# Buffers, order and lag operations in a fused attention and feed-forward layer on one core

## The chip, the cores and the metric

The kernel runs on one core of one Trainium2 chip. A core has five engines that run their own instruction lists: TensorE (PE in the profile, with PEld for its weight loads), VectorE (DVE), ScalarE (ACT), GpSimd (POOL) and SyncE (SP). POOL and SP issue nearly all transfers here; SP's queue is written SPq. The metric is the device time of one execution in microseconds. Before the change the median of three executions was 1432.9 us (1429.92 to 1437.33).

## The reference

One layer over 2048 tokens of width 512, all in float32. After a layer norm come a short recurrent attention with 16 heads of 128 and a feed-forward part with weights reduced to their signs, and both meet at the end.

```python
q = _silu(x @ Wq); k = _silu(x @ Wk); v = _silu(x @ Wv)
z = x @ Wz; a = x @ Wa; b = x @ Wb
q, k, v = (_causal_dwconv(u, w) for u, w in ...)      # 4 taps
q = q * cos + rot_half(q) * sin                       # k likewise
q = q / jnp.maximum(jnp.linalg.norm(q, axis=-1, keepdims=True), 1e-12)   # k likewise
for s in range(4):                                    # lags
    attn = jnp.einsum('bshd,bshd->bsh', q, _lag(k, s)) * scale
    gate = jax.nn.sigmoid(_lag(a, s) * b)
    out = out + (attn * gate)[..., None] * _lag(v, s)
rms = jax.lax.rsqrt(jnp.mean(out * out, axis=-1, keepdims=True) + EPS_NORM)
s = (out * rms * norm_w * _silu(z)) @ Wout
hidden = jax.nn.relu((xn @ sign(up).T) * up_scale)
g = _silu((hidden @ sign(down).T) * down_scale * output_scale)
return x + s * g
```

## The kernel before

Tokens lie along the free axis, channels on the 128 partitions. The 2048 tokens are four blocks of 512 (`b`, `TB`), the 16 heads eight pairs (`p`, `NP`); a pair is 256 channels, two tiles `j` of 128. The normalised and transposed input `xnT` of all blocks stays in SBUF, each row with three zero columns ahead of it (`HALO`), for the lags.

`step(p, b)` (L604) is the unit of work. It computes q and k of pair p for block **b + 1** (`queries`, `products`) and v, z and the output of pair p for block **b**. So the first pass, b = -1, has only q and k, and beside them runs the feed-forward part of block 0 (`ups`, `downs`), whose raw weights are loaded, turned into signs and stored for later (`fetch`, L699). The last block (L765 to L828) has only v, z and the output, in a loop of its own, and behind it comes the feed-forward part of blocks 1 to 3.

For a pair, PE multiplies `xnT` by the pair's weights (16 records of a 128x512 matmul for each of q, k, v, z, under the names pq, pk, pv, pz), ACT takes the SiLU out of PSUM into a "raw" tile, ACT and DVE apply the four taps (`convolve`, L322: one ACT multiply at L325 and three DVE operations per half). `turn` makes from q the three turned copies for lags 1 to 3; `products` (L366) multiplies them by k at four shifts (`pr`), and PE sums over channels into a PSUM bank "dots" (`sum_dots`). The squares of q and k go the same way into "squares" (`sum_squares`).

Once per block, at p = 0, `norms` (L469) takes the squares out of PSUM into `r`, via a copy `sq2` (L475); `norms_in_rows` (L482) takes reciprocals and spreads them by eight small DMAs on SP into `rk` and `rq`; `coefficients` (L496) multiplies dots, norms and gates, and stores them in DRAM (`co_dram`). `gate_products` (L231, at p = 7) and `gate` (L251, at p = 1) prepare the gates: PE makes four partial sums, ACT copies them to `ab_sb`, and POOL adds them in DRAM by a chain of four DMAs (L247, L249), each waiting for the one before; sixteen DMAs on SP bring them back. The tiles ab_sb, gate_b, sq2 and rk share **one** buffer, tag "rk".

`weighted` (L525) brings the coefficients back from DRAM, repeated over partitions (`bc`, two lags to a tile, three buffers), multiplies them with v at four shifts and adds (`te`, `o`). `gated_output` (L556) multiplies with z (`oz`), and for every two pairs `output_projection` (L570) adds four PSUM tiles (po) to the result in DRAM. At p = 0 the output of the pair (`out_of`) is put off to the next step, in `first_due`, since its coefficients have just been computed; its z is not.

The order of work: PE and DVE keep the order of the program text (the wrapper `InOrder`), and so does POOL for the add of squares, and SP in the last block. What is left on ACT, SP and POOL is ordered by the framework's planner before the program runs. Every engine then works its list in order, so an instruction that waits holds all behind it. Buffers are given per tag; with `bufs=1` the next writer waits for the last reader of the same tag.

Of the kernel before, what the change touches and what calls it, by code (L numbers as in the profile page):

```python
# [38 lines left out]
F32 = mybir.dt.float32  # L39
# [5 lines left out]
P = 128  # L45
# [36 lines left out]
def recurrent_layer(ctx: ExitStack, tc: tile.TileContext, a: dict, out: bass.AP):  # L82
# [148 lines left out]
    def gate_products(b):  # L231


        chunks = mm.tile([P, TB], F32, tag="mm", name=f"ab{b}")
        for k in range(KC):
            pe.matmul(
                chunks[LW * k : LW * k + LW, :],
                w_ab[:, k, :],
                xnT[:, k, HALO + b * TB : HALO + (b + 1) * TB],
                start=True,  # L240
                stop=True,
                tile_position=(0, LW * k),
            )
        ab = qks.tile([P, TB], F32, tag="rk", name=f"ab_sb{b}", bufs=1)
        nc.scalar.copy(ab, chunks)
        to = ab_dram[:, HALO + b * TB : HALO + (b + 1) * TB]
        nc.gpsimd.dma_start(to, ab[0:LW, :])  # L247
        for k in range(1, KC):
            nc.gpsimd.dma_start(to, ab[LW * k : LW * k + LW, :], accum_op=ALU.add)  # L249

    def gate(b):  # L251

        g = qks.tile([P, TB], F32, tag="gate", name=f"gate{b}", bufs=1)
        other = qks.tile([P, TB], F32, tag="rk", name=f"gate_b{b}", bufs=1)
        for r in range(0, P, H):
            lo = HALO + b * TB - r // LW
            nc.sync.dma_start(g[r : r + H, :], ab_dram[0:H, lo : lo + TB])
            nc.sync.dma_start(other[r : r + H, :], ab_dram[H:, HALO + b * TB : HALO + (b + 1) * TB])
        dve.tensor_tensor(g, g, other, ALU.mult)
        nc.scalar.activation(g, g, AF.Sigmoid)  # L260
        gates[b] = g
# [104 lines left out]
    def products(p, b, q, between=None, beside_k=None):  # L366
# [43 lines left out]
        if not b:  # L410
# [35 lines left out]
    def sum_dots():  # L446
# [4 lines left out]
        for pr in prs:  # L451
            for s in range(LAGS):
                src = pr[:, LAGS - 1 - s, :]
                add(banks["dots"], s, heads, src, p == 0, last and pr is prs[-1])

    def sums_of_o(b):

        so = mm.tile([P, TB], F32, tag="mm", name=f"so{b}")
        for j in range(2):
            add(so, j, ones, squares[b][:, j], True, True)  # L460
        row = vs.tile([P, HID], F32, tag="part", name=f"so_sb{b}", bufs=3)
        nc.scalar.copy(row[0 : 2 * LW], so[0 : 2 * LW])  # L462
# [6 lines left out]
    def norms(b):  # L469

        sqs = banks["squares"]
        r = qks.tile([P, HALO + TB], F32, tag="r", name=f"r{b}", bufs=1)[0 : 2 * LW]
        nc.scalar.copy(r[0:LW, 0:HALO], kept_r)
# [8 lines left out]
    def norms_in_rows(b):  # L482
# [7 lines left out]
        for s in range(LAGS):  # L490
            at = slice(LW * s, LW * s + LW)
            nc.sync.dma_start(rq[at, :], r[LW :, HALO:])
            nc.sync.dma_start(rk[at, :], r[0:LW, HALO - s : HALO - s + TB])
        rows[b] = rk, rq
# [12 lines left out]
    def values(p, b, raw):  # L507
# [4 lines left out]
        return v  # L512

    def load_wo(p, b):
        wo = vs.tile([P, 2, HID], F32, tag="wo", name=f"wo_{p}_{b}", bufs=3)
        loads["by"].dma_start(wo, a["wo"][p])
        return wo

# [6 lines left out]
    def weighted(p, b, v):  # L525

        n = f"_{p}_{b}"
        o = vs.tile([P, 2, TB], F32, tag="o", name="o" + n, bufs=1)
        for s in range(LAGS):
            if s % 2 == 0:  # L530

                bc = vs.tile([P, 2, TB], F32, tag="bc", name=f"bc{s}" + n, bufs=3)
                for h in range(2):
                    row = co_dram[b][s : s + 2, 2 * p + h, :]
                    loads["by"].dma_start(
                        bc[h * D // 2 : (h + 1) * D // 2], row.partition_broadcast(D // 2)
                    )
            b2 = bc[:, s % 2].unsqueeze(1).to_broadcast([P, 2, TB])
            v_s = v[:, :, HALO - s : HALO - s + TB]
            if s == 0:  # L540
                dve.tensor_tensor(o, v_s, b2, ALU.mult)
            else:
                te = vs.tile([P, 2, TB], F32, tag="te", name=f"te{s}" + n, bufs=2)
                dve.tensor_tensor(te, v_s, b2, ALU.mult)
                dve.tensor_tensor(o, o, te, ALU.add)

# [9 lines left out]
    def gated_output(p, b, o, z, wo):  # L556
# [6 lines left out]
        gated[p] = oz, wo  # L563
        if p % 2 == 1:
            pairs = gated.pop(p - 1), gated.pop(p)
            outputs_due.append(lambda midway: output_projection(p, b, midway, *pairs))
        if p == NP - 1:
            outputs_due.append(lambda midway: sums_of_o(b))

    def output_projection(p, b, midway, *pairs):  # L570

        for c in range(TC):
            if midway and c == TC // 2:
                midway()
            po = mm.tile([P, HID], F32, tag="mm", name=f"po{c}_{p}_{b}")
            for i, (of, w) in enumerate(pairs):
                for j in range(2):
# [23 lines left out]

    first_due = []

    def step(p, b, beside_q=None, beside_k=None):  # L604
# [30 lines left out]
        if at:  # L635
            load(vs, "z", p, b)
            wo = load_wo(p, b)
            z = gates_of_output(p, b)
            out_of = lambda: gated_output(p, b, weighted(p, b, v), z, wo)
# [39 lines left out]

    def up_projection(ph, pool, f, b, up_f, xs):  # L680
        for k in range(KC):
            for i, term in enumerate(xs):
# [6 lines left out]
                )  # L689
        hid = pool.tile([P, TB], F32, tag="hid", name=f"hid{f}_{b}", bufs=3)  # L690
        nc.scalar.activation(hid, ph, AF.Relu, scale=up_scale[:, f : f + 1])  # L691
# [4 lines left out]
    with tc.tile_pool(name="pre", bufs=1, side="right") as pre:  # L696
        signs = {}

        def fetch(g, which):  # L699

            for f in range(G * g, G * g + G):
                raw = pre.tile([P, HID], F32, tag="raw", name=f"pre_{which}_raw{f}", bufs=4)
                src = a[which][f]
                nc.sync.dma_start(raw, src.rearrange("p k m -> p (k m)") if which == "up" else src)
                sign = pre.tile([P, HID], F32R, tag="sign", name=f"pre_{which}{f}", bufs=8)

                (act if f < G else nc.scalar).activation(sign, raw, AF.Sign)
                nc.gpsimd.dma_start(signs_dram[which][:, f], sign)
                signs[which, f] = sign

        hids = {}

        def ups(lo, hi):
            for f in range(lo, hi):
                up_f = signs.pop(("up", f)).rearrange("p (k m) -> p k m", k=KC)
                ph = mm.tile([P, TB], F32, tag="mm", name=f"ph{f}")
                hids[f] = up_projection(ph, pre, f, 0, up_f, xs)

# [57 lines left out]
    load(vs, "v", 2, last)  # L776
    wo = load_wo(0, last)
    sum_dots()
# [21 lines left out]
    for p in range(NP + 1):  # L800
        if 1 < p < NP:
            weights["v"] = v_weights.pop(p)
            raw = raw_of(vs, "v", p, last, 1)
        if p:
            z = gates_of_output(p - 1, last)
# [9 lines left out]
        if p:  # L815
            gated_output(p - 1, last, o, z, wo)
# [211 lines left out]
```

## Time and profile before

| what | value |
|---|---|
| median of three runs | 1432.9 us |
| the profiled execution | 1432.86 us, span 1431.1 us |
| PE | 1405.0 us busy (98%), 3970 matmul records |
| DVE | 1209.8 us busy (85%), 1363 instructions |
| ACT | 611.6 us busy (43%) |
| POOL | 231.2 us busy (16%) |
| mean granted PE clock | 0.994 |

The span is the time from the first to the last instruction. An engine's busy time counts its instructions, not its waits. In the lists below "idle before <-releaser" is the time that the engine stood before an instruction, and what ended it. One logical float32 matmul shows as two records. The slices of the page, in tenths of 1/40 of the span, show PE full nearly throughout and DVE nearly so until the last quarter:

```profile
PE   9999999799999999999999999999998999999998
...
DVE  7899988999999979999999899999995978246454
```

### The profile page before, as it was taken

The numbers are of one execution on the slowest core, as the hardware profiler recorded it, in microseconds if no ns is written. First come the engines' busy times: TensorE is split into PE (matmuls) and PEld (weight loads), VectorE is DVE, ScalarE is ACT, GpSimd is POOL, SyncE is SP. The second block draws the span as 40 slices with busy tenths as digits, with TensorE's granted clock in tenths as the row PEclk, the third lists the DMA queues.
The fourth block names the chain that finished last, engine by engine and source line by source line (L and its number), as shares of the span: only waits on it lengthen the run. The fifth ranks groups of instructions, "written<-read, shape, count | busy, mean of one in ns | idle before, by whom it ended". The sixth has DMA issues, their size and how long they took to land.

```text
span 1431.1 us, 12627 instructions
## 1 busy us (share of the span) xinstructions
PE 1405.0 (98%) x3970; PEld 689.1 (48%) x3970; DVE 1209.8 (85%) x1363; ACT 611.6 (43%) x1181; POOL 231.2 (16%) x317
## 2 busy tenths in 40 slices
PE   9999999799999999999999999999998999999998
PEld 5554544344444444444444444444443444478886
DVE  7899988999999979999999899999995978246454
ACT  6575545445444443444434444444442333232122
POOL 2222120111212220112122201121211111200000
PEclk9999999999999999999999999999999999999999
DMA  9979576987998588779986798797748878662120
GB/s 308 269 194 213 151 198 139 228 211 185 192 220 198 135 176 235 199 167 203 214 201 150 165 238 194 179 204 175 167 87 219 221 209 200 130 232 89 33 88 30
DMA packets 101778, 259.22 MB, mean 181 GB/s; under 512 B 18832, under 2 KB 19344, under 8 KB 97360
## 3 DMA queue, kind: packets, MB, share of 16 engines
q0 software_dynamic: 33088, 104.89, 38.4%
q1 hardware_dynamic: 68624, 153.53, 35.5%
q8 instruction: 32, 0.52, 0.1%
q14 instruction: 34, 0.28, 0.1%
HBM read 157.67 MB, written 35.68 MB: 135 GB/s over the span
## 4 chain that ended last, share of the span: by engine, by line
PE 64%; DVE 20%; issue 7%; DMA 5%; ACT 2%; SPq 1%; POOL 1%; DVEq 0%; POOLq 0%; ACTq 0%
PE po L76 13%; PE pz L76 11%; PE pv L76 9%; PE pq L76 8%; PE pk L76 8%; PE pf L76 6%; PE ph L76 6%; DVE q L76 4%; DVE pr L76 3%; DVE k L76 2%; DVE te L76 2%; DVE o L76 2%; DVE v L76 2%; DMA ab_dram<-ab_sb 1%; DMA gate_b<-ab_dram 1%
## 5 line engine op out<-in xcount | busy, mean ns | idle before, releaser
L76 PE MATMUL po<-wo,oz 128*128 128x512 f32 x512 | 228.8, 601 | 10.5 <-DVE oz L76 10.5
L76 PE MATMUL pz<-xnT,wz 128*128 128x512 f32 x512 | 228.3, 599 | 4.5 <-DMA wz<-in_wz_dram 4.5
L76 PE MATMUL pq<-xnT,wq 128*128 128x512 f32 (+1 forms) x528 | 226.1, 580 | 0.9 <-ACT rk L274 0.9
L76 PE MATMUL pv<-xnT,wv 128*128 128x512 f32 x512 | 226.4, 594 | 0.0
L76 PE MATMUL pk<-xnT,wk 128*128 128x512 f32 x512 | 225.2, 592 | 0.0
L76 PEld LDWEIGHTS po<-wo,oz 128*128 128x128 f32 x512 | 97.0, 192 | 139.6 <-issue 112.7
L76 DVE SCALAR_TENSOR_TENSOR k<-rk,conv_w,k 128x512 f32<-128x512 f32 x192 | 141.9, 751 | 24.3 <-ACT k L325 19.8
L76 PEld LDWEIGHTS pz<-xnT,wz 128*128 128x128 f32 x512 | 97.4, 191 | 131.0 <-issue 128.9
L76 DVE SCALAR_TENSOR_TENSOR q<-rq,conv_w,q 128x512 f32<-128x512 f32 x192 | 141.3, 749 | 22.2 <-ACT q L325 17.7
L76 PEld LDWEIGHTS pq<-xnT,wq 128*128 128x128 f32 x528 | 99.0, 189 | 124.1 <-issue 115.2
L76 PEld LDWEIGHTS pv<-xnT,wv 128*128 128x128 f32 x512 | 95.7, 189 | 127.7 <-issue 117.8
L76 PEld LDWEIGHTS pk<-xnT,wk 128*128 128x128 f32 x512 | 96.6, 189 | 120.5 <-issue 116.9
L76 DVE SCALAR_TENSOR_TENSOR v<-rv,conv_w,v 128x512 f32<-128x512 f32 x192 | 141.3, 750 | 5.5 <-ACT v L325 1.0
L76 DVE SCALAR_TENSOR_TENSOR q<-q,turns 128x1024 f32<-128x1024 f32 (+1 forms) x128 | 127.1, 1013 | 2.3
L76 DVE TENSOR_TENSOR o<-o,te 128x1024 f32<-128x1024 f32 x96 | 117.6, 1225 | 3.3
L76 DVE TENSOR_TENSOR te<-v,bc 128x1024 f32<-128x1024 f32 x96 | 116.9, 1218 | 1.9 <-DMA bc<-co_dram 1.9
L76 DVE TENSOR_TENSOR pr<-q,k 128x2048 f32<-128x2048 f32 x52 | 117.3, 2286 | 0.9
L691 ACT ACTIVATE hid<-ph,up_scale 128x512 f32<-128x512 f32 x64 | 43.8, 685 | 120.0 <-PE ph L76 119.4
L76 DVE CAST hid_hi<-hid 128x512 fp32r<-128x512 f32 x64 | 27.1, 423 | 71.9 <-ACT hid L691 71.9
L76 PE MATMUL ph<-xs_hi,up 128*128 128x512 f32 x192 | 76.4, 398 | 0.7 <-ACT so_sb L462 0.7
L76 PE MATMUL ph<-xs_lo,up 128*128 128x512 f32 x192 | 75.9, 395 | 0.0
L586 ACT COPY part<-po 128x512 f32<-128x512 f32 x64 | 37.1, 581 | 90.4 <-PE po L76 53.7
(146 smaller groups left out, 1663.0 us busy)
## 6 DMA issues: line engine op xcount, KB each, us to landing
bc<-co_dram SPq DMA_DIRECT2D x128, 256.0 KB, 6.8
pr<-pr POOLq DMA_DIRECT2D x72, 256.0 KB, 6.0
wq<-in_wq_dram SPq DMA_DIRECT2D x32, 512.0 KB, 6.7
wk<-in_wk_dram SPq DMA_DIRECT2D x32, 512.0 KB, 6.6
sq<-sq POOLq DMA_DIRECT2D x32, 512.0 KB, 5.7
wv<-in_wv_dram SPq DMA_DIRECT2D x32, 512.0 KB, 6.1
wz<-in_wz_dram SPq DMA_DIRECT2D x32, 512.0 KB, 5.1
wo<-in_wo_dram SPq DMA_DIRECT2D x32, 512.0 KB, 6.5
```

The costliest lines, as they stand in the source:

```text
L76: return self.tc.keep_in_program_order(getattr(self.engine, op)(*args, **kwargs))
L586: nc.scalar.copy(part, po)
L691: nc.scalar.activation(hid, ph, AF.Relu, scale=up_scale[:, f : f + 1])
```

## The change

**Own buffers.** `ab_sb` gets its own tag "ab" instead of "rk". `r` gets two buffers instead of one, `part` (and the row of squares that shares it) four instead of three. `hid` gets two instead of three in the feed-forward part of blocks 1 to 3.

**z of a first pair.** At p = 0 the matmuls of z are no longer issued in step 0, but in step 1, between k and v (`z_due`).

**Two lags in one operation.** The four lags are stored in reverse (row group s holds lag 3 - s), so that two lags of v are one access pattern. `weighted` multiplies two lags at once and adds the two results in place; the square `o2` goes into a part of `xnT` that is no longer read, or (block 0) into the place of the second product. In `products` the second half of an odd pair is one multiply in place over q and one add, instead of two of each.

**Signs.** `fetch` only loads, into eight buffers instead of four, two steps ahead; `sign` makes the signs a step ahead.

**Last block.** z's weights of pair 1 are loaded before the coefficients are computed. The first output product moves from the third to the fourth turn of the loop, behind z of pair 3; wo of pairs 3 and 4 are then loaded together.

```diff
-        ab = qks.tile([P, TB], F32, tag="rk", name=f"ab_sb{b}", bufs=1)
+        ab = qks.tile([P, TB], F32, tag="ab", name=f"ab_sb{b}", bufs=1)
...
-            lo = HALO + b * TB - r // LW
+            lo = b * TB + r // LW
...
-            for lo in range(0, LAGS, 2):
-                half = qks.tile([P, 2, TB], F32, tag="half", name=f"half{lo}" + n, bufs=1)
-                product(half, 1, lo, lo + 2)
-                dve.tensor_tensor(pr[:, lo : lo + 2], pr[:, lo : lo + 2], half, ALU.add)
+            product(q[:, :, 1], 1, 0, LAGS)
+            dve.tensor_tensor(pr, pr, q[:, :, 1], ALU.add)
...
-        r = qks.tile([P, HALO + TB], F32, tag="r", name=f"r{b}", bufs=1)[0 : 2 * LW]
+        r = qks.tile([P, HALO + TB], F32, tag="r", name=f"r{b}", bufs=2)[0 : 2 * LW]
...
     def weighted(p, b, v):
...
+            v0 = v[:, :, lo : lo + TB]
+            v_lags = bass.AP(v0.tensor, v0.offset, [v0.ap[0], [1, 2], *v0.ap[1:]])
+            te = vs.tile([P, 2, 2, TB], F32, tag=f"te{lo}", name=f"te{lo}" + n, bufs=1)
+            dve.tensor_tensor(te, v_lags, bc.unsqueeze(2).to_broadcast([P, 2, 2, TB]), ALU.mult)
+            parts.append(te)
+        dve.tensor_tensor(parts[0], parts[0], parts[1], ALU.add)
+        o = parts[0][:, 0]
+        dve.tensor_tensor(o, o, parts[0][:, 1], ALU.add)
...
-            o2 = vs.tile([P, 2, TB], F32, tag="o2", name="o2" + n, bufs=1)
+            o2 = xnT[:, p % 2 * 2 : p % 2 * 2 + 2, HALO : HALO + TB] if b else parts[1][:, 0]
...
-            part = vs.tile([P, HID], F32, tag="part", name=f"part{c}_{p}_{b}", bufs=3)
+            part = vs.tile([P, HID], F32, tag="part", name=f"part{c}_{p}_{b}", bufs=4)
...
         products(p, b + 1, q, (lambda: norms_in_rows(b)) if change and b else None, beside_k)
+        if z_due:
+            z_due.pop()()
...
             if change:
+                z_due.append(z_of)
                 first_due.append(out_of)
             else:
+                z_of()
                 out_of()
...
-    def up_projection(ph, pool, f, b, up_f, xs):
+    def up_projection(ph, pool, f, b, up_f, xs, bufs=2):
...
-                raw = pre.tile([P, HID], F32, tag="raw", name=f"pre_{which}_raw{f}", bufs=4)
+                raw = pre.tile([P, HID], F32, tag="raw", name=f"pre_{which}_raw{f}", bufs=8)
...
+        groups = [(g, which) for g in range(NP // 2) for which in ("up", "down")]
+        fetch(*groups[0])
+        def first_signs():
+            sign(*groups[0])
+            fetch(*groups[1])
...
-                step(p, -1, lambda: fetch(0, "up"), lambda: ups(0, G))
+                step(p, -1, first_signs, lambda: ups(0, G))
...
-            if p < NP - 1:
-                fetch((p + 1) // 2, "down" if p % 2 == 0 else "up")
+            if p + 1 < NP:
+                sign(*groups[p + 1])
+            if p + 2 < NP:
+                fetch(*groups[p + 2])
...
-    wo = load_wo(0, last)
+    load_wo(0, last)
+    z_weights = {0: weights["z"]}
+    load(vs, "z", 1, last)
+    z_weights[1] = weights["z"]
     sum_dots()
     coefficients(last)
...
-        if p % 2 == 1:
+        if p % 2 == 1 and p != 3 or p == 4:
             output_projections()
+        if 1 < p < NP:
+            load(vs, "z", p, last)
+            z_weights[p] = weights["z"]
         if 0 < p < NP:
-            load(vs, "z", p, last)
             v = values(p, last, raw)
...
-        if 0 < p < NP:
-            wo = load_wo(p, last)
+        if p == 4:
+            load_wo(3, last)
+        if 0 < p < NP and p != 3:
+            load_wo(p, last)
```

More of the change, by code (lines that the diff above doesn't have):

```diff
@@ L452, in sum_dots @@
             for s in range(LAGS):
-                src = pr[:, LAGS - 1 - s, :]
-                add(banks["dots"], s, heads, src, p == 0, last and pr is prs[-1])
+                add(banks["dots"], s, heads, pr[:, s, :], p == 0, last and pr is prs[-1])
     def sums_of_o(b):
@@ L460, in sums_of_o @@
             add(so, j, ones, squares[b][:, j], True, True)
-        row = vs.tile([P, HID], F32, tag="part", name=f"so_sb{b}", bufs=3)
+        row = vs.tile([P, HID], F32, tag="part", name=f"so_sb{b}", bufs=4)
         nc.scalar.copy(row[0 : 2 * LW], so[0 : 2 * LW])
@@ L492, in norms_in_rows @@
             nc.sync.dma_start(rq[at, :], r[LW :, HALO:])
-            nc.sync.dma_start(rk[at, :], r[0:LW, HALO - s : HALO - s + TB])
+            nc.sync.dma_start(rk[at, :], r[0:LW, s : s + TB])
         rows[b] = rk, rq
@@ L512, in values @@
         return v
+    wos = {}
     def load_wo(p, b):
@@ L516, in load_wo @@
         loads["by"].dma_start(wo, a["wo"][p])
-        return wo
+        wos[p] = wo
     def gates_of_output(p, b):
@@ L527, in weighted @@
         n = f"_{p}_{b}"
[L528 to L545, printed above, removed]
+        parts = []
+        for lo in range(0, LAGS, 2):
+            bc = vs.tile([P, 2, TB], F32, tag="bc", name=f"bc{lo}" + n, bufs=3)
+            for h in range(2):
+                row = co_dram[b][lo : lo + 2, 2 * p + h, :]
+                loads["by"].dma_start(
+                    bc[h * D // 2 : (h + 1) * D // 2], row.partition_broadcast(D // 2)
+                )
+            v0 = v[:, :, lo : lo + TB]
[6 more added lines that the diff above has]
+        dve.tensor_tensor(o, o, parts[0][:, 1], ALU.add)
         if p == 0:
@@ L554, in weighted, with gated_output @@
         return o
-    def gated_output(p, b, o, z, wo):
+    def gated_output(p, b, o, z):
         oz = vs.tile([P, 2, TB], F32, tag="oz", name=f"oz_{p}_{b}", bufs=3)
@@ L562, in gated_output, with output_projection @@
             )
-        gated[p] = oz, wo
+        gated[p] = oz
         if p % 2 == 1:
             pairs = gated.pop(p - 1), gated.pop(p)
-            outputs_due.append(lambda midway: output_projection(p, b, midway, *pairs))
+            outputs_due.append(lambda midway: output_projection(p, b, midway, pairs))
         if p == NP - 1:
             outputs_due.append(lambda midway: sums_of_o(b))
-    def output_projection(p, b, midway, *pairs):
+    def output_projection(p, b, midway, pairs):
+        ws = wos.pop(p - 1), wos.pop(p)
         for c in range(TC):
@@ L575, in output_projection @@
             po = mm.tile([P, HID], F32, tag="mm", name=f"po{c}_{p}_{b}")
-            for i, (of, w) in enumerate(pairs):
+            for i, (of, w) in enumerate(zip(pairs, ws)):
                 for j in range(2):
@@ L602, in recurrent_layer @@
     first_due = []
+    z_due = []
     def step(p, b, beside_q=None, beside_k=None):
@@ L636, in step @@
             load(vs, "z", p, b)
-            wo = load_wo(p, b)
-            z = gates_of_output(p, b)
-            out_of = lambda: gated_output(p, b, weighted(p, b, v), z, wo)
+            load_wo(p, b)
+            z = []
+            z_of = lambda: z.append(gates_of_output(p, b))
+            out_of = lambda: gated_output(p, b, weighted(p, b, v), z[0])
             if change:
+                z_due.append(z_of)
                 first_due.append(out_of)
             else:
+                z_of()
                 out_of()
@@ L689, in up_projection @@
                 )
-        hid = pool.tile([P, TB], F32, tag="hid", name=f"hid{f}_{b}", bufs=3)
+        hid = pool.tile([P, TB], F32, tag="hid", name=f"hid{f}_{b}", bufs=bufs)
         nc.scalar.activation(hid, ph, AF.Relu, scale=up_scale[:, f : f + 1])
@@ L697, in recurrent_layer, with sign @@
         signs = {}
+        raws = {}
         def fetch(g, which):
             for f in range(G * g, G * g + G):
-                raw = pre.tile([P, HID], F32, tag="raw", name=f"pre_{which}_raw{f}", bufs=4)
+                raw = pre.tile([P, HID], F32, tag="raw", name=f"pre_{which}_raw{f}", bufs=8)
                 src = a[which][f]
                 nc.sync.dma_start(raw, src.rearrange("p k m -> p (k m)") if which == "up" else src)
[L705 to L709, printed above, removed]
+                raws[which, f] = raw
+        def sign(g, which):
+            for f in range(G * g, G * g + G):
+                of = pre.tile([P, HID], F32R, tag="sign", name=f"pre_{which}{f}", bufs=8)
+                (act if which == "up" and f < G else nc.scalar).activation(
+                    of, raws.pop((which, f)), AF.Sign
+                )
+                nc.gpsimd.dma_start(signs_dram[which][:, f], of)
+                signs[which, f] = of
         hids = {}
@@ L716, in ups @@
                 ph = mm.tile([P, TB], F32, tag="mm", name=f"ph{f}")
-                hids[f] = up_projection(ph, pre, f, 0, up_f, xs)
+                hids[f] = up_projection(ph, pre, f, 0, up_f, xs, 3)
         def downs(g, lo, hi):
@@ L804, in recurrent_layer @@
         if p:
+            weights["z"] = z_weights.pop(p - 1)
             z = gates_of_output(p - 1, last)
-        if p % 2 == 1:
+        if p % 2 == 1 and p != 3 or p == 4:
             output_projections()
+        if 1 < p < NP:
+            load(vs, "z", p, last)
+            z_weights[p] = weights["z"]
         if 0 < p < NP:
-            load(vs, "z", p, last)
             v = values(p, last, raw)
@@ L815, in recurrent_layer @@
         if p:
-            gated_output(p - 1, last, o, z, wo)
+            gated_output(p - 1, last, o, z)
         if p < NP:
             o = weighted(p, last, v)
-        if 0 < p < NP:
-            wo = load_wo(p, last)
+        if p == 4:
+            load_wo(3, last)
+        if 0 < p < NP and p != 3:
+            load_wo(p, last)
         if p < NP:
```

## The prediction

> **What bounds the kernel now.** I read the page's shares first (PE 98% busy, DVE 85%), then the stage table, which gives each engine's busy time in stretches that I cut at the same point of the loop (its columns: stretch, length, busy time and count of PE, PEld, DVE, ACT and POOL, granted clock, DMA share, GB/s).
>
> ```profile
> 209.00:300.00 91.00, 83.74 (x217) 34.91 (x217) 82.86 (x93) 42.24 (x87) 11.07 (x15) 0.94 0.76 192
> 371.50:442.50 71.00, 71.00 (x177) 30.35 (x177) 69.35 (x72) 30.96 (x64) 13.28 (x17) 1.00 0.97 211
> 515.70:589.20 73.50, 71.64 (x179) 30.62 (x178) 63.49 (x75) 32.93 (x68) 11.59 (x16) 1.00 0.79 209
> 1084.70:1161.00 76.30, 71.83 (x162) 31.39 (x161) 56.43 (x61) 21.68 (x40) 9.31 (x14) 0.96 0.82 217
> ```
>
> A stretch of two pairs (second row) is 71.0 us of PE in 71.0 us, with DVE only 1.65 us behind. The change takes no matmul away, so it can win only what PE loses: 7.26 us in the first block, 1.86 in the second, 4.47 in the last, and a clock below 1 in two of these stretches. PE's own list of waits and its order of time show where:
>
> ```profile
> PE po L76 <- DVE oz L76: 10.5, 3, 7.3
> PE pz L76 <- DMA wz<-in_wz_dram: 4.5, 1, 4.5
> ...
> 284.30 7.20 PE L76 MATMUL po<-wo,oz 128*128 128x512 f32 x10 [7.26 <-DVE oz L76]
> 575.70 1.55 PE L76 MATMUL po<-wo,oz 128*128 128x512 f32 x3 [1.86 <-DVE oz L76]
> 1103.19 9.92 PE L76 MATMUL pz<-xnT,wz 128*128 128x512 f32 x16 [4.47 <-DMA wz<-in_wz_dram]
> 1112.95 7.03 PE L76 MATMUL pv<-xnT,wv 128*128 128x512 f32 x16
> ```
>
> Sixteen records take 7.03 us at full rate, 0.43 each. After the 7.26 us wait ten take 7.20, that is 2.9 too many; after 4.47 us sixteen take 9.92, again 2.9; after 1.86 us three take 1.55, nothing extra. A long wait is paid twice. **What PE loses:** 7.26 + 2.9 = 10.2 (first block), 1.86 and 1.39 (second and third, the three waits of 10.5), 4.47 + 2.9 = 7.4 (last block), and 2.45 at 131 us, where five starts of pf that should be 0.233 apart cover 3.62 us behind hid_hi. Sum 23.3. That is the ceiling.
>
> **Who is late.** In the first three, oz comes from DVE, which runs its list in order without a gap up to the stall; so its last idle time before it counts. The orders of time of DVE and ACT:
>
> ```profile
> 217.57 2.33 DVE L76 SCALAR_TENSOR_TENSOR k<-rk,conv_w,k 128x512 f32<-128x512 f32 x3 [5.46 <-ACT k L325]
> 216.23 0.58 ACT L475 COPY sq<-squares 64x512 f32<-64x512 f32 x1 [4.69 <-DMA ab_dram<-ab_sb]
> ...
> 517.25 0.19 ACT L473 COPY r<-kept_r 32x3 f32<-32x3 f32 x1 [5.25 <-DMA rk<-r]
> 526.33 0.60 ACT L313 ACTIVATE rq<-pq 128x512 f32<-128x512 f32 x1 [2.84 <-PE pq L76]
> 527.72 2.33 DVE L76 SCALAR_TENSOR_TENSOR q<-rq,conv_w,q 128x512 f32<-128x512 f32 x3 [4.55 <-ACT q L325]
> ```
>
> At 216 ACT stands before sq2 (L475), whose buffer, tag "rk", is still read by the gates' sums (L249, a chain of POOL adds, the last landing at 216.05). k's second half is queued behind it, and DVE idles 5.46. At 527 it is PE's order: z of pair 0 stands ahead of q of pair 1, so DVE starves 4.55, then 1.58, 0.64 and 1.57 until k is through, 8.3 in all.
>
> **Part by part.**
>
> *Own buffer for ab; r twice; part four times.* ab off "rk" frees L475: rk's second copy ends at 211.54, kept copy 0.20 and multiply 0.72 bring k to 212.4, DVE is free at 212.1; 0.3 of the 5.46 stays, DVE gains 5.2. The copy into r (L473) no longer waits (14.0 us in three waits), nor part on s_dram (30.0 in three); they hold ACT's queue, and no PE wait names them: counted as nothing. Without that cover the nearest price is the 5.46 of the same kind.
>
> *z behind next k.* The 16 records of z (6.87 us) trade places with q and k of pair 1; v of pair 1 starts when it did. DVE gets q 6.87 sooner: the 8.3 us go, and in the third block 3.17 + 1.48 + 1.83 = 6.5. z is needed by the first oz, 560.4 in the second block; PE would finish it at 536.4. What is late next is bc of pair 0, landing by 539.6; DVE now reaches it at 551.9, then at 543.6. Waits of 1.86 and 1.39 need only that much: **3.25** gained, bounds 0 and 3.25.
>
> *Two lags in one operation.* Rows for it:
>
> ```profile
> L76 DVE TENSOR_TENSOR o<-o,te 128x1024 f32<-128x1024 f32 x96 | 117.6, 1225 | 3.3
> L76 DVE TENSOR_TENSOR pr<-q,k 128x2048 f32<-128x2048 f32 x52 | 117.3, 2286 | 0.9
> L76 DVE TENSOR_TENSOR te<-v,bc 128x1024 f32<-128x1024 f32 x96 | 116.9, 1218 | 1.9 <-DMA bc<-co_dram 1.9
> ```
>
> Before, a pair takes four multiplies and three adds of 1024, 4 x 1.22 + 3 x 1.225 = 8.56. After: two multiplies of 2048 at pr's 2.286, an add of 2048 (2.29), one of 1024: 8.09. An odd pair's four halves (4.89) become 2 x 2.29 = 4.57. DVE saves 0.47 a pair and 0.32 an odd pair, 32 x 0.47 + 12 x 0.32 = 19 us in all, and the end gets none of it directly, since PE is full; in the first block's chain it is 2 x 0.47 + 0.32 = 1.3 sooner. No row shows a multiply that reads v at two shifts and repeats bc: below, pr's 2.286 (it reads k at four shifts); above, twice that. I take 2.286, by shape the nearest. Reversed lag order costs nothing (same instructions). q comes free after 4.57 instead of 3.67 us; twelve us of v and weighted stand on DVE before its next use. o2 in the second product's place (block 0) must have been added before the next pair's second multiply: the slowest add landed at 410.8, that multiply is due at 416.0; if late, DVE pays the difference, and it has 1.65 us.
>
> *First block, summed.* oz's first half ended 284.25; minus 5.2 and 1.3 it is 277.75, and PE asks at 276.87: a wait of 0.9 remains, too short for the second price. Gain **9.3**, bounds 7 (wait of 3, no slow stretch) and 10.2.
>
> *Signs sooner.* ACT stood 5.50 at 39.6 and 4.62 at 71.5 for raw weights. From DVE's idle time behind them (1.73, 1.41, 0.67) only what comes after 54 us reaches the stall at 131, since k at 54.0 is paced by PE: 0.67, and some 0.6 for a square that held k. Of 2.45 it wins **1.2**, bounds 0 and 2.45. The four loads per group move past wq and wk on SP; wq of pair 1 landed at 20.8 and is used near 32, which hides their 1 MB; POOL's stores of the signs stay behind their signs.
>
> *Last block's loads.* The queue of SP, in order:
>
> ```profile
> 1081.65 0.43 SPq L76 DMA_DIRECT2D wo<-in_wo_dram  x1
> 1085.03 0.33 SPq L503 DMA_DIRECT2D co_dram<-rk  x1
> 1089.82 2.61 SPq L76 DMA_DIRECT2D bc<-co_dram  x4
> 1092.47 0.59 SPq L76 DMA_DIRECT2D wz<-in_wz_dram  x1
> 1093.16 0.67 SPq L76 DMA_DIRECT2D wv<-in_wv_dram  x1
> ```
>
> wz of pair 1 is behind the coefficients' store and four bc; it lands at 1103.06, PE asks at 1098.6. Moved up it goes out near 1082.2 (v1's buffer is free since 1068.6), with 2.8 us of empty queue before the store, and has 16 us: **7.4** gained. Next are wv3, landed 1105.51, asked for at 1105.4, and wz2, 1111.98 against 1112.3; both then have 0.5 MB less ahead of them. The first output product would have met its oz (1125.84) 6 us too early; moved behind z3 it is asked for at 1132.9. wo3 and wo4 then wait for its end, 1146.6, with z5, v7 and bc5 queued behind; po of pairs 2 and 3 asks at 1160.4, and a wo takes 6.5 to land. v7 waits for z4's buffer till 1160.4 anyhow. Bounds 0 and 7.4.
>
> [...]
>
> *hid twice instead of three times in the feed-forward part:* DVE is idle 2.5 of each 3.73 us there, and two buffers cover 7.46: nothing.
>
> **Sum:** 9.3 + 3.25 + 7.4 + 1.2 = 21.1. The profiled execution took 1432.86 (span 1431.1, 1.76 around it), the median is 1432.9, so no correction: 1432.9 - 21.1 = **1411.8**.
>
> [...]
>
> **Rivals.** *The first block's stall survives:* with L475 free, DVE meets the next late thing (bc of pair 0, landing 252.3 to 255.4, moves with co_dram only if the rows of rq and rk do). For: SP issues eight row copies and twelve gate copies there in line. Against: each follows DVE's own earlier end. 1411.8 + 9.3 = 1421.
>
> *The waits only move on:* wv3 and wz2 come late in wz's place (margins 0.1 and 0.3 us), and the first block stalls as before. Then 3.25 + 1.2 remain: 1428.5. For: what is not pinned, on ACT and SP, the planner may lay out anew. Against: the queue loses half a megabyte just before them.
>
> *Slower: DVE becomes the bound through the combined multiply.* In the ten stretches from 300 to 1019.6 DVE is busy 677.5 of 719.6, so 42 us are free, and the change saves 13 there. The 40 multiplies begin to cost in the tightest stretch (1.65 idle) from 3.0 us each; they eat the whole gain at (42 + 13 + 21) / 40 = 1.9 more, 4.2 each. At twice pr's row, 4.57: 40 x 2.29 - 55 = 36 over, 1448. For: no row shows this reading. Against: from 1024 to 2048 elements pr and te's own rows grow alike.
>
> **Chances.** Forecast 0.68 (its own range 1407 to 1417); first stall survives 0.13; waits move on 0.09; slower 0.10. About 0.5%, 7 us, is what a measurement here can tell from no change: the first two lie below 1425.7, so faster 0.81, same 0.09, slower 0.10. The range goes from the ceiling (1432.9 - 23.3 = 1409.6, less 0.3% of spread) to past the first rival: 1405 to 1424.
>
> **What would show it.** Right: no idle time before po near 276 over 2 us, none near 575 and 864, pz at 1098.6 without a wait, clock 1.00 in both stretches, te at 2.29. Wrong: te above 3.0; a new releaser at one of these places; a wait on wv or wz after 1100; ACT standing before a copy for a DMA near 216.

## The result and the profile after

The changed kernel took 1411.65 us (median of six runs, 1410.65 to 1412.05) against 1432.84 us for the kernel before in the same job (six runs, 1429.92 to 1437.33). The ratio is 0.9848, 95% interval 0.983 to 0.9866. The profiled execution took 1412.02 us, with a span of 1410.2, and the mean granted clock of TensorE rose from 0.994 to 0.999.

The stage table of the changed kernel, cut at the same points of the loop as before (stretch, length, busy time and count of PE, PEld, DVE, ACT and POOL, granted clock, DMA share, GB/s):

```profile
206.50:289.10 82.60, 81.05 (x216) 33.88 (x217) 79.33 (x83) 43.93 (x87) 11.00 (x15) 1.00 0.84 210
360.60:431.60 71.00, 71.00 (x177) 30.36 (x176) 68.80 (x64) 30.21 (x64) 16.88 (x21) 1.00 0.94 215
504.80:576.10 71.30, 71.30 (x179) 30.65 (x178) 66.85 (x70) 34.03 (x68) 11.92 (x16) 1.00 0.93 219
1070.00:1140.00 70.00, 69.46 (x162) 30.13 (x161) 54.07 (x48) 21.01 (x40) 10.38 (x14) 1.00 0.94 226
```

The full stretch in the second row is as long as before, to the hundredth. The first has become 8.4 us shorter, the third 2.2, the last 6.3, and the clock is 1.00 in all of them. PE's list of waits (time in all, times, longest) and its order of time in the changed kernel:

```profile
PE po L76 <- DVE oz L76: 1.6, 1, 1.6
PE pz L76 <- ACT rv L313: 0.5, 1, 0.5
...
276.02 5.42 PE L76 MATMUL po<-wo,oz 128*128 128x512 f32 x12 [1.55 <-DVE oz L76]
1083.86 7.03 PE L76 MATMUL pz<-xnT,wz 128*128 128x512 f32 x16
1098.30 7.14 PE L76 MATMUL pz<-xnT,wz 128*128 128x512 f32 x16 [0.54 <-ACT rv L313]
```

One of the three waits on oz is left, 1.55 us where there were 7.26, and the 12 records behind it run at full rate. The wait on wz is gone, and z of the next pair waits 0.54 us for something new, ACT's work on rv. ACT and DVE at the places where DVE had run dry (ACT first, then DVE):

```profile
208.99 0.58 ACT L473 COPY sq<-squares 64x512 f32<-64x512 f32 x1
...
210.33 2.33 DVE L76 SCALAR_TENSOR_TENSOR k<-rk,conv_w,k 128x512 f32<-128x512 f32 x3 [0.80 <-ACT k L325]
516.33 2.33 DVE L76 SCALAR_TENSOR_TENSOR q<-rq,conv_w,q 128x512 f32<-128x512 f32 x3 [1.41 <-ACT q L325]
522.30 2.33 DVE L76 SCALAR_TENSOR_TENSOR k<-rk,conv_w,k 128x512 f32<-128x512 f32 x3 [1.41 <-ACT k L325]
```

The copy of the squares goes at once instead of standing 4.69 us, DVE's 5.46 has become 0.80, and of the 8.3 us of the second block twice 1.41 is left. The groups of the weighted sum show what its new operations cost:

```profile
L76 DVE TENSOR_TENSOR te<-v,bc 128x2048 f32<-128x2048 f32 x64 | 143.9, 2288 | 19.4 <-DMA bc<-co_dram 18.1
L76 DVE TENSOR_TENSOR te<-te,te 128x2048 f32<-128x2048 f32 x32 | 73.3, 2292 | 1.1
```

2.288 us for two lags, against 2.286 for the multiply of the same size in pr: reading v at two shifts and repeating bc costs nothing here. The queue of SP at the start of the last block:

```profile
1065.94 0.39 SPq L76 DMA_DIRECT2D wz<-in_wz_dram  x1
1069.13 0.33 SPq L501 DMA_DIRECT2D co_dram<-rk  x1
1075.92 2.61 SPq L76 DMA_DIRECT2D bc<-co_dram  x4
1078.63 0.54 SPq L76 DMA_DIRECT2D wv<-in_wv_dram  x1
```

wz goes out 3.2 us ahead of the store of the coefficients. bc is issued when that store has landed, 6.79 us after its issue; before the change it was 4.79.

**Where the time came from.** The start of the same matmul record in both traces gives the gain up to there. At q of pair 4 in the first pass (171.8 before) it is 2.45 us; behind the first block (300.3) 10.92; behind the second (589.0) 13.04; behind the third (877.3) 14.70; behind the start of the last (1161.0) 20.95, and to the end nothing is added.

| place | booked | measured |
|---|---|---|
| pf near 131 | 1.2 | 2.45 |
| po near 276 | 9.3 | 8.47 |
| po near 575 and 864 | 3.25 | 2.12 + 1.66 = 3.78 |
| last block | 7.4 | 6.25 |
| sum | 21.1 | 20.95 |

### The profile page after: what moved, and what is told of

The parts are those of the page before. It is cut to its first block, busy times and chain, and to the rows that moved or that the text cites. A ratio compares the mean times of both kernels' runs of the same rounds, so it can differ in the third digit from the quotient of the medians.

```text
span 1410.2 us, 12492 instructions
## 1 busy us (share of the span) xinstructions
PE 1399.2 (99%) x3970; PEld 687.7 (49%) x3970; DVE 1197.2 (85%) x1243; ACT 610.3 (43%) x1181; POOL 237.3 (17%) x317
## 4 chain that ended last, share of the span: by engine, by line
PE 58%; DVE 28%; DMA 5%; issue 4%; ACT 3%; SPq 1%; POOL 0%; DVEq 0%; ACTq 0%; POOLq 0%
PE pq L76 9%; DVE q L76 8%; PE pk L76 8%; PE ph L76 8%; PE pf L76 8%; PE pz L76 8%; PE po L76 8%; DVE te L76 7%; PE pv L76 6%; DVE v L76 4%; DVE k L76 4%; DVE pr L76 3%; DMA bc<-co_dram 2%; DMA co_dram<-rk 1%; PE dots L76 1%
## 5 line engine op out<-in xcount | busy, mean ns | idle before, releaser
L76 PE MATMUL po<-wo,oz 128*128 128x512 f32 x512 | 225.9, 595 | 1.6 <-DVE oz L76 1.6
L76 PE MATMUL pz<-xnT,wz 128*128 128x512 f32 x512 | 225.3, 592 | 0.5 <-ACT rv L313 0.5
L76 DVE TENSOR_TENSOR te<-v,bc 128x2048 f32<-128x2048 f32 x64 | 143.9, 2288 | 19.4 <-DMA bc<-co_dram 18.1
L76 DVE TENSOR_TENSOR te<-te,te 128x2048 f32<-128x2048 f32 x32 | 73.3, 2292 | 1.1
L594 POOL DMA_DIRECT2D s_dram<-part x48 | 50.7, 1231 | 70.1 <-ACT part L588 66.5
```

The costliest lines, as they stand in the source:

```text
L76: return self.tc.keep_in_program_order(getattr(self.engine, op)(*args, **kwargs))
L594: nc.gpsimd.dma_start(rows, part, accum_op=ALU.add)
```

## The experiments

The places are right; the question was whether each gain came from the edit that it had been booked to. Seven kernels take one edit out of the changed kernel, one takes out two, three put one edit alone into the kernel before, and one tries to go further. Runs 4 and 9 are less clean than that; each says why. The median of a run stands against 1411.65; the ratio is to the kernel before in the same job. Waits and times of a place are those of each kernel's profiled execution.

**1. The gates' sums share a buffer again.**

```diff
-        ab = qks.tile([P, TB], F32, tag="ab", name=f"ab_sb{b}", bufs=1)
+        ab = qks.tile([P, TB], F32, tag="rk", name=f"ab_sb{b}", bufs=1)
```

> The kernel after with one thing undone: ab_sb shares tag rk again. Theory (the shared buffer made the first block's stall): ACT stands before sq2 near 212 us for the gates' sums again, DVE idles some 5.2 us before k's second half, and the wait of po near 276, 1.55 us after the change, becomes 6.7 us with some 2.9 us of slow matmuls behind it: 1411.7 + 5.2 + 2.9 = 1419.8. Rival (z's new place and the fewer DVE operations did it): within 1 us of 1411.7.

Measured: 1417.68 us (1416.83 to 1418.66), ratio 0.9894 [0.9863, 0.9925]. The stall comes back, at another place. ACT's and PE's order of time in this kernel:

```profile
212.40 0.58 ACT L473 COPY sq<-squares 64x512 f32<-64x512 f32 x1 [3.95 <-DMA ab_dram<-ab_sb]
...
268.30 7.92 PE L76 MATMUL pv<-xnT,wv 128*128 128x512 f32 x11 [3.08 <-DMA wv<-in_wv_dram]
```

ACT stands before the same copy as in the kernel before. The copy is 3.4 us later than in the changed kernel, the store of the coefficients 2.9 (236.55 against 233.66), and wv, behind bc in SP's queue, 3.1 (260.40 against 257.31). PE then waits 3.08 us for wv, and 11 records take 7.92 us instead of 4.9. So the shared buffer was a cause of the first block's stall, but with the other edits in place its lateness reaches PE through SP's queue sooner than through oz. By the starts of the same records 4.3 us are lost in the first block and 2.6 more in the last, where z waits 1.93 for ACT instead of 0.54 and four records run at half rate.

**2. z of a first pair in its old place** (`z_of()` called in step 0 again).

> The kernel after with z of a first pair back in its own step. Theory (z's place removed the stalls at 575 and 864): DVE idles before q and k of pair 1 again, 8.3 and 6.5 us; the waits of 1.86 and 1.39 us come back less the 1.3 us that the fewer DVE operations save before them, 0.6 and 0.1, and in the first block k of pair 1 comes some 1.5 us late: 1412.4 to 1414. First rival, as booked in the prediction (nothing else helps there): 1411.7 + 3.25 = 1414.9 or more. Second rival (the other parts alone remove these stalls): 1411.7 and no wait of po near 565 and 855.

Measured: 1414.06 us (1411.98 to 1414.47), ratio 0.9867 [0.9841, 0.9893]. po waits again in the second and third block, 0.81 and 0.35 us, and z in the last block 1.52 for ACT instead of 0.54. The edit does what it was booked for, though of the 3.25 us of waits only 1.16 come back while the other edits stand.

**3. One lag at a time in the weighted sum.** The products keep their merged form.

```diff
-            te = vs.tile([P, 2, 2, TB], F32, tag=f"te{lo}", name=f"te{lo}" + n, bufs=1)
-            dve.tensor_tensor(te, v_lags, bc.unsqueeze(2).to_broadcast([P, 2, 2, TB]), ALU.mult)
-            parts.append(te)
+            for i in range(2):
+                b2 = bc[:, i].unsqueeze(1).to_broadcast([P, 2, TB])
+                dve.tensor_tensor(te[:, i], v[:, :, lo + i : lo + i + TB], b2, ALU.mult)
+                if lo or i:
+                    dve.tensor_tensor(parts[0][:, 0], parts[0][:, 0], te[:, i], ALU.add)
```

> The kernel after with four multiplies of 1024 and three adds of 1024 per pair again in the weighting by lags (8.56 us of DVE in place of 8.09). Theory (PE is full, so DVE's 15 us count only in the first block's chain): po near 276 waits 0.94 us longer, 2.5 in place of 1.55: 1412.6, no other wait of PE. Rival (DVE bounds in part): more than 3 us, with new waits of PE in the blocks.

Measured: 1415.7 us (1414.14 to 1417.47), ratio 0.9882 [0.9855, 0.9909]; more than expected. The first block's wait grew from 1.55 to 2.16, and four records behind it now run at half rate, 1.7 us more. Two waits in the last block are new. From PE's waits in this kernel:

```profile
PE po L76 <- DVE oz L76: 2.2, 1, 2.2
PE pz L76 <- ACT z L313: 2.0, 1, 2.0
...
PE pv L76 <- DMA wv<-in_wv_dram: 0.9, 1, 0.9
```

So by the starts of the same records a DVE that is later by half a microsecond a pair costs 2.3 us in the first block, and 2.2 in the last, where the prediction had booked nothing.

**4. Signs' weights loaded late again** (four raw buffers, `fetch` and `sign` at one place). This isn't quite the code of the kernel before. There, each sign followed its own load, and the signs of the first group of `down` were held in program order; here four loads come before four signs, and this line of the change stays, which leaves `down` to the planner:

```diff
-                (act if f < G else nc.scalar).activation(sign, raw, AF.Sign)
+                (act if which == "up" and f < G else nc.scalar).activation(
```

> The kernel after with raw weights loaded and turned into signs at the same place, four buffers, as before. Theory by the result (early loads removed the whole stall of pf near 131): pf waits there again and loses 2.45 us, the wait of po near 276 changes by less than 1 us: 1414.1. As booked in the prediction (only half of the stall): 1412.9. Rival (the stall went for another reason): 1411.7.

Measured: 1419.34 us (1416.48 to 1419.71), ratio 0.9903 [0.9876, 0.993]; far more than expected. The profiled execution, the fastest at 1416.48, shows pf waiting for hid_hi 0.94 us at 41.7 and 1.66 at 135.8; with the slower records behind them they cost 1.6 and 3.1. The wait at 41.7 isn't in the kernel before. ACT in that kernel (first line), then ACT and PE in this one:

```profile
33.41 0.69 ACT L691 ACTIVATE hid<-ph,up_scale 128x512 f32<-128x512 f32 x1 [0.57 <-DVE hid_lo L76]
...
40.00 0.63 ACT L722 ACTIVATE pre_up<-pre_up_raw 128x512 fp32r<-128x512 f32 x1 [1.78 <-DMA pre_up_raw<-in_up_dram]
40.53 0.67 ACT L700 ACTIVATE hid<-ph,up_scale 128x512 f32<-128x512 f32 x1
...
41.74 0.50 PE L76 MATMUL pf<-pre_down,hid_hi 128*128 128x512 f32 x1 [0.94 <-DVE hid_hi L76]
```

The planner has put the last hid behind four signs that wait for their loads, so it comes 7 us later. The run prices late loads together with that order, and not the edit alone. Where the other runs lost 3 us more no trace shows.

**5. The last block's first weights of z loaded in the loop again**, behind the coefficients' store and bc.

```diff
-    load(vs, "z", 1, last)
-    z_weights[1] = weights["z"]
...
-        if 1 < p < NP:
+        if 0 < p < NP:
             load(vs, "z", p, last)
```

> The kernel after with z's weights of pair 1 loaded in the last block's loop again, the first output product still at the fourth turn. Theory: PE waits for wz near 1077 to 1082 us, some 4.5 us, and loses 2.9 more at a lower clock: 1411.7 + 7.4 = 1419.1. Rival (the wait is covered by what else changed, or moves on to other loads anyway): within 1 us of 1411.7.

Measured: 1411.65 us (1410.94 to 1417.35), ratio 0.9857 [0.9831, 0.9883]: the median is the same as with the edit, though one of the four executions took 1417.35. SP's queue and PE in this kernel:

```profile
1068.80 0.33 SPq L501 DMA_DIRECT2D co_dram<-rk  x1
1072.37 2.60 SPq L76 DMA_DIRECT2D bc<-co_dram  x4
1075.02 0.59 SPq L76 DMA_DIRECT2D wz<-in_wz_dram  x1
...
1083.51 7.11 PE L76 MATMUL pz<-xnT,wz 128*128 128x512 f32 x16
```

pz runs almost without a wait, with wz in its old place behind bc. This falsifies the step on the load: 7.4 us had been booked to it, and without it the median loses nothing. But there is no margin. The traced execution is the fastest of the four; in it wz lands at 1083.37, and pz starts 0.25 us later than full rate would have it. Whether the execution of 1417.35 met the wait no trace shows.

In the kernel before, wz landed 18.0 us after the store's issue, and PE asked for it 13.5 after it. Here it lands 14.6 after the store's issue, and PE asks at 14.5. So of the vanished wait some 1 us is a store that comes sooner against PE, and 3.5 are shorter transfers: the store 1.2, the load of wz 2.2 (8.36 us instead of 10.58). Why that load is shorter no run shows. What shortened the wait is the question of runs 8 to 11. The store of the coefficients is seen here without wz beside it: 3.57 us, against 6.79 with it.

**6. The first output product back in the third turn of the last loop.**

```diff
-        if p % 2 == 1 and p != 3 or p == 4:
+        if p % 2 == 1:
             output_projections()
```

> The kernel after with the first output product back at the third turn of the last block's loop, z's weights still early. Theory (without the move the 7.4 us would turn into a wait for oz of pair 1): po waits some 6 us near 1110 and loses 2.9 more: 1411.7 + 9 = 1420.6. Rival (DVE is early enough, the move is not needed): within 1 us of 1411.7.

Measured: 1418.1 us (1417.76 to 1420.88), ratio 0.9898 [0.9878, 0.9917]. PE in this kernel:

```profile
1111.24 11.10 PE L76 MATMUL po<-wo,oz 128*128 128x512 f32 x22 [5.00 <-DVE oz L76]
```

The product meets its oz 5.00 us too early, and its first records run at half rate, 1.5 us in all: 6.5 lost. Of the last block's edits this one is needed, at least while z no longer waits.

**7. One buffer of r, three of part, three of hid**, as before.

> The kernel after with one buffer for r, three for part and three for hid again. Theory (these waits hold ACT alone, no wait of PE names them): 1411.7 within 0.7. Rival (ACT's copy into r stands up to 7.7 us and holds what DVE needs for q and k of pair 1): new waits of po near 565 and 855, 1 to 4 us more.

Measured: 1412.34 us (1412.02 to 1412.88), ratio 0.9854 [0.9836, 0.9871]: 0.7 us, if anything. Its trace has z at 1098.8 waiting 1.63 us for the weights of pair 2, where the changed kernel waits 0.54 for ACT; what these buffers have to do with it is not shown.

**8. The lags and z's load both back** (the edits of runs 3 and 5).

> The changed kernel with two parts undone at once: the weighted sum again takes one lag at a time (two multiplies of 1.22 us and an addition each instead of one multiply of 2.29 us per two lags), and the last block's first weights of z are loaded in its loop again. With the load alone put back, z of the last block found its weights in time. Theory A: what had made z wait 4.47 us for its weights before was the vector engine, late with the last full block, which put the norms, the coefficients and every load behind them some 2 us later against TensorE; then with the lags apart the wait for wz is back: 2 to 4.5 us at about 1100 us in the trace, no wait that ends on z's activation in its place, and the time is that of the lags put back alone (1415.7) give or take 1.5 us. Rival B: the buffers, or the order in which parts are stored, made the weights late; then there is no wait for wz over 0.5 us, and the time is 1413 to 1414.

Measured: 1413.95 us (1412.37 to 1416.49), ratio 0.9877 [0.9851, 0.9904]. SP's queue and PE in this kernel, whose profiled execution is the longest of its four, 1416.49:

```profile
1071.83 0.33 SPq L501 DMA_DIRECT2D co_dram<-rk  x1
1076.26 2.60 SPq L76 DMA_DIRECT2D bc<-co_dram  x4
1078.91 0.59 SPq L76 DMA_DIRECT2D wz<-in_wz_dram  x1
...
1087.53 8.80 PE L76 MATMUL pz<-xnT,wz 128*128 128x512 f32 x16 [2.57 <-DMA wz<-in_wz_dram]
```

The wait for wz is back, and 16 records take 8.80 us instead of 7.03. Against run 5 only the lags differ. There pz starts 14.7 us after the store's issue (1068.80 to 1083.51), here it is asked for 13.1 after it (1071.83 to 1087.53, less the wait of 2.57): the coefficients are 1.6 us later against PE, and the store takes 4.43 instead of 3.57. These two make up nearly all of the wait. Since run 5 had no margin, a DVE that is late by the lags is enough to bring it back. The wait is the one that theory A asks for, and the traced execution lies in its range. The median does not: with 1413.95 it is in rival B's, and the three other executions (1412.37, 1412.94, 1414.96) left no trace. So the lags can bring the wait back, and it is not shown that they always do.

**9. The lags alone in the kernel before.**

> The kernel before with only the lags changed (reversed order of lags, both products of keys and queries and the weighted sum in one operation for several lags); shared buffers, z's place, the signs and the last block's loads as before. Theory A: the last block's 4.47 us and the 2.9 us of slow matmuls behind it are gone or under 1.5 us together, and the waits of 1.85 and 1.4 us at 572 and 860 shrink below 1 us; the first block's 7.26 us of waiting stays, shorter by what the vector engine saves before the shared buffer's release (5 to 7.3 us). Sum: 1432.9 - 6 to 7.4 - 1 to 2 - 0 to 2 = 1422 to 1426. Rival B: nothing but the two shorter waits goes: 1430 to 1432.

Measured: 1430.05 us (ten runs, 1427.07 to 1434.4), ratio 0.9987 [0.9972, 1.0002]: no gain that can be told. But the kernel isn't the kernel before with the lags alone: it has run 4's order of loads and signs too. PE's waits in this kernel:

```profile
PE po L76 <- DVE oz L76: 7.8, 4, 5.2
PE pf L76 <- DVE hid_hi L76: 2.7, 2, 2.0
PE pz L76 <- DMA wz<-in_wz_dram: 2.1, 1, 2.1
```

Each expected step is there: wz 4.47 to 2.14, without records at half rate behind it; po in the second and third block 1.86 and 1.39 to 0.82 and 0.34; the first block 7.26 to 5.23. But pf now waits 1.98 us at 42, where it did not before, with 1.7 us of half rate behind it, and po in the last block 1.36 at 1125. The wait at 42 is that of run 4, with the last hid at 40.83 behind four signs, and DVE idle 5.38 us for it, so this trace puts it to the order of the signs and not to a faster DVE. At 172 us the same records start 4.9 us later than in the kernel before, and at the end 2.8 sooner. So behind the first pass this trace gains 7.7 us: 2.3 in the first block, 1.0 in each of the next two, and 5.1 at wz less 1.6 at po in the last. If the first pass lost nothing, the time would by this estimate be near 1424 (1431.9 for the kernel before in this job), in theory A's range and not in rival B's. A run of the lags without the signs' order was not made.

**10. The own buffer for the gates' sums alone in the kernel before.**

> The kernel before with the own buffer for ab_sb alone. Theory: DVE gains 5.2 us in the first block, the wait of po at 276 falls from 7.26 to 2.1 us and the slow matmuls behind it go, 8.1 us in all: 1432.8 - 8.1 = 1424.7; the waits at 575, 864 and 1103 stay. Rival (the next late thing takes over): the wait stays above 5 us, 1430 or more.

Measured: 1428.5 us (six runs, 1426.92 to 1431.0), ratio 0.9963 [0.9947, 0.9979]. The first block's wait falls from 7.26 to 2.58 us, still with 1.7 us of half rate; wz waits 3.61. pf waits for hid_hi 0.90 us at 86, which is new, and 1.40 at 135; PE is 1.9 us behind the kernel before when the first pass ends. Raw weights for the signs land later there (41.39 against 39.51), which the edit doesn't explain. The mechanism is right; alone it takes 4.7 us off the wait and 1.2 off what follows it, and some of that is lost again at pf.

**11. z behind k alone in the kernel before.**

> The kernel before with z of a block's first pair behind the next block's first projection of k, and nothing else. Prediction's reading: the waits at 575 and 864 (3.25 us in all) go, the first block's and the last block's stay as they were: 1429.6 (1428.5 to 1431). Rival: z behind k takes nothing from them, since the vector engine still comes late with one lag at a time, and the wait turns up behind z: 1432 to 1434.

Measured: 1432.83 us (ten runs, 1429.55 to 1435.19), ratio 1.0002 [0.9988, 1.0017]. PE in this kernel:

```profile
276.62 8.62 PE L76 MATMUL pv<-xnT,wv 128*128 128x512 f32 x16 [5.98 <-ACT k L325]
...
1068.96 1.93 PE L76 MATMUL dots<-pr,of_heads 128*32 128x512 f32 x8 [3.04 <-DMA pr<-pr]
```

The waits at 575 and 864 are gone, as booked. The first block's stall only moves from po to pv, and what PE gained, 3.3 us, is lost before the last block: dots wait 3.04 us for a sum that POOL's transfers add up (pr<-pr), which lands no sooner than before, and 2.9 us of half rate follow. The first pass loses 2.4 us at pf, as in run 10. Alone the edit is worth nothing.

**12. Sums of squares next to sums of dots: a try to go on.** In the changed kernel's trace TensorE loses some 0.33 us at each visit from matmuls of 128 columns to those of 32 and back.

```diff
-        if p % 2 == 0:
-            sum_squares()
...
-        output_projections(sum_dots if due else None)
+        def sums_due():
+            sum_dots()
+            if len(squares_due) > 2:
+                sum_squares()
+        output_projections(sums_due if due else None)
```

> The changed kernel with the sums of squares of two pairs taken next to the sums of dots in the same step (a third buffer for the squares; one buffer fewer for the norms' rows and the parts, which cost 0.7 us when put back alone, to make room). It saves 12 visits of TensorE from matmuls of 128 columns to those of 32 and back. In the trace the start-to-start times round one visit of 8 records are 0.52, 0.45, 0.54 and 0.53 us against 0.43 between two full matmuls in a row: 0.33 us a visit. Theory: 12 x 0.33 = 4.0 us less, 0.7 us more for the buffers: 1408.3 (1407 to 1409.5), faster than both. Rival: the visit costs the same wherever it stands, or the squares' later release stops the scalar engine: 1412 to 1415.

Measured: 1411.62 us (1410.39 to 1414.6), ratio 0.9862 [0.9836, 0.9889]: the same as the changed kernel. The size was right: between the full matmuls on either side, a visit of 8 records covers 2.05 us of starts and one of 16 covers 2.91, of which 0.86 are two full records; 2 x 1.19 - 2.05 = 0.33 saved each. From the end of the first block to the start of the last PE gains 2.7 us over the changed kernel, 8 x 0.33. PE's and SP's order of time in this kernel (PE first):

```profile
267.41 2.81 PE L76 MATMUL pv<-xnT,wv 128*128 128x512 f32 x6 [2.30 <-ACT rv L274]
1090.09 7.11 PE L76 MATMUL pv<-xnT,wv 128*128 128x512 f32 x16 [0.78 <-DMA wv<-in_wv_dram]
1099.31 8.83 PE L76 MATMUL pz<-xnT,wz 128*128 128x512 f32 x16 [2.11 <-ACT rv L313]
...
1069.50 0.33 SPq L499 DMA_DIRECT2D co_dram<-rk  x1
1076.90 2.60 SPq L76 DMA_DIRECT2D bc<-co_dram  x4
```

PE comes to the last block 1.6 us sooner, but the coefficients are stored at 1069.50, not sooner than 1069.13 in the changed kernel. All that is gained waits there, and more: this trace, the longest of the four, ends 2.6 us behind the changed kernel's. In it the last block is set by the chain through DVE, the coefficients' store and bc, and the first by DVE, which works without a gap up to 267; neither by PE's own work. No version was found that beats the changed kernel; this one together with run 5's load was not tried.

## Why the prediction was right, and where its reasons were not

**The sum** was off by 0.2 us (1411.8 against 1411.65), and each place by at most 1.25 us. That is partly luck: 1.25 too little near 131 and 0.5 at 575 and 864 stand against 0.8 too much in the first block and 1.15 in the last.

**Where TensorE loses time, and what a wait costs with the records behind it**: right. The full stretch did not move, and all of the gain lies at the five waits named. Only the bound with a wait of 3 us and no slow records is not borne out: the waits of 2.57 to 3.08 in these traces all had them.

**First block**: the buffer that ACT stood before is a cause, shown by taking it away in both directions (runs 1 and 10). The end of oz was booked for 277.75 with 0.9 us of wait left; 1.55 was left. The step's sum needs more than the buffer: alone it leaves 2.58 and the half rate behind it, and the lags alone leave 5.23.

**z behind k**: "Waits of 1.86 and 1.39 need only that much: 3.25 gained" is right by place, and run 2 brings part of them back. But run 11 shows that the term counts only while the rest is mended too: alone, the first block's stall moves to pv, and the 3.3 us gained are lost at dots. That the waits only move on, one of the rivals, is what happens to this edit alone, though not at the loads that the rival named.

**Two lags in one operation**: the price, 2.286 a multiply, was exact (2.288), and the slower rival fell with it. "The end gets none of it directly" is the step that was mis-sized: taken out again, the lags cost some 4 us (run 3): 2.3 in the first block, where 1.3 had been booked, and 2.2 in the last, where nothing had. The last block starts from what DVE has finished.

**Signs sooner**: booked at 1.2, the lower half of its bounds; all of the 2.45 went. Only the part of DVE's idle time behind 54 us had been counted. Run 4 loses 5 to 8 us without the early loads, but it keeps part of the edit, an order of signs that is worse with late loads, so it is no price for this term; 3 us of it no trace explains.

**Last block's loads**: the step that failed. "Moved up it goes out near 1082.2 ... and has 16 us: 7.4 gained" is true of the transfer and wrong about the gain. Run 5 leaves the load where it was and its median loses nothing, if only just, since wz lands as PE asks for it; in the traced execution of run 8 the wait is back once the lags are undone as well, and in run 9 2.3 of the 4.47 and the half rate behind it go without the load. What the prediction had wrong is that wz in its old place would be as late as before: in run 5 the store comes some 1 us sooner against PE, and the store and the load of wz together take 3.5 us less. Why that load is shorter stays open. Early loading is a second cure for the same wait: it gives a margin, and it has a price. From its issue to the issue of bc, the store of the coefficients took 6.7 to 7.4 us with wz beside it (the changed kernel and runs 3, 7 and 12), and 3.6 to 4.9 without it (the kernel before and runs 5, 8, 9 and 10). The changed kernel's 6.79 is 2.0 more than in the kernel before and 3.2 more than in run 5. The move of the first output product, booked together with the load, costs 6.5 when it alone is undone (run 6). What remained of wz's wait besides the lags was not split further: alone, the own buffer leaves 3.61 and z behind k 2.68, and in the latter PE is also late.

**Nothing for r, part and hid**: within 0.7 us (run 7).

## What to carry to other kernels

When an engine is full between a few waits, the list of waits with what follows each of them is the whole gain, and it can be read off before; which edit removes which wait can't, since one early chain can cure several. So undo each edit in the new kernel and also put it alone into the old one: here z behind k is worth 2.4 us in one and nothing in the other, and the moved load nothing in the median where 7.4 had been booked. Undo an edit down to the order of its lines: runs 4 and 9 kept a part of another one and so can't price what they were made for. Before saving time on the full engine, look at whether the next block's start is released by it at all.

## What the runs showed of the hardware that was not expected

**A short wait can be paid twice.** In the prediction waits up to 1.86 us were free and 4.47 dear, with nothing between. Over all traces twelve waits of PE between 1.36 and 1.86 us before po, pv or pz left the next records 0.43 us apart. Waits of 1.93, 2.11 and 2.16 us were followed by some four intervals of 0.85, which cost 1.7 us, and so were those of 2.57, 2.58 and 2.68, while waits of 2.02, 2.14, 2.15 and 2.30 us were followed by none. After 3.08, 3.61, 4.47 and 7.26 the price was 2.7 to 3.0, after 5.23 it was 2.4, and after 5.00 and 5.98 only 1.4 to 1.5.

The granted clock shows where the price comes from. In the kernel before it was 0.50 for 10.24 us from 279.42, which is 2.38 us into the wait of 7.26, and for 6.83 us from 1102.03, 3.31 us into the wait of 4.47. In the changed kernel, whose longest wait before po, pv or pz is 1.55 us, it was 1.00 from 7.8 us to 1407. In both cases of the kernel before, the price is about half of what is left of the slow stretch when PE starts again: 5.36 us after the wait of 7.26, which cost 2.7, and 5.67 after that of 4.47, which cost 2.9. Between 1.93 and 2.30 us the length of a wait doesn't tell whether it is paid twice; what does is not shown.

**Narrow matmuls have a price at their edges.** Eight records of 32 columns among full ones cost 1.19 us of PE's time and sixteen together 2.05, so a visit costs 0.33 us beyond its work (the traces of the changed kernel and of run 12).
